# A sandwich of a linear recurrence and a mixture of experts on one core: the softmax's exponentials move from GpSimd to ScalarE, and the first slots are put in another order

## The chip, the cores and the metric

The kernel runs on one core of a Trainium2 chip. The metric is the device time of one execution in microseconds (us); lower is better. The engines are called PE (TensorE, matmuls; PEld is its weight loads), DVE (VectorE), ACT (ScalarE), POOL (GpSimd) and SP (SyncE, which issues most DMAs). Each engine runs its own instructions in the order in which the program has them, and waits for others by semaphores.

## What is computed

The input is 16 blocks of 512 rows and 128 features, all float32. The reference, cut to what matters here:

```python
x = x + layernorm(attn(layernorm(x)))       # per block: Bu = x B^T, a causal convolution along the
                                            # 512 rows with complex eigenvalues, C, and D * x
x = x + layernorm(ffn(layernorm(x)))

# ffn, E = 8 experts, F = 512:
router_probs = softmax(x @ w_router)                 # 8 values for each row
gate_weights = softmax((x @ w_gating) / 0.1)         # 8 values for each row
g = x @ w_gate[e];  u = x @ w_up[e]
out_e = (silu(g) * u) @ w_down[e]
cw = router_probs * gate_weights;  cw = cw / (sum(cw) + 1e-9)
out = sum over e of out_e * cw[e]
```

The softmax of the two routers is what the change touches: for each block of 512 rows it takes 4 x 2 x 8 exponentials in each of 128 partitions.

## The kernel before

**Tiling.** A block is 512 rows, held as 4 chunks of 128. For the experts the features lie on the partitions and the 512 rows along the free dimension. A *slot* is one of the four 128-wide pieces of F of one expert of one block: 4 x 8 = 32 slots a block, 512 slots in all, numbered n. A product of float32 accuracy is made of three matmuls (`mm3`, L337): high part by high part (L338), low part of the weights by high part (L339), and high part by low part (L340). So a slot has nine matmuls of 512 columns: three for g, three for uu (`up`, L554) and, four slots later (LAG), three for d (`down`, L589).

**What the other engines do in a slot.** ACT takes the silu of g from PSUM (`sg`, L564). DVE multiplies it by uu (`gate`, L575); the product stays in uu's PSUM bank, or goes to `hh` in SBUF. ACT rounds the product to its high part (`hi`, L580), and the low part is the difference (`lo`, L586): on DVE, or on POOL where `lo_pool[n]` says so (then the product is in `hh`). Every fourth slot DVE multiplies an expert's d by its combine weights (`ct`, L606) and POOL adds it to the sum (`acc`, L609). PSUM has two banks for g and three for uu, so g(n + 2) can start only after silu(n) has read its bank, and uu(n + 3) only after uu(n) has been read.

**Beside them.** While the slots of one block run, the next block's front part (`front`: two layer norms, the recurrence by a scan on DVE at L381, matmuls bu and yp on PE) and its `route` run as generators, a step at a time, and so does the end of the block before (`back`, with its layer norm and the store). The generator says with each `yield` after how many slots the next step may come and what it costs on DVE, ACT and POOL. In each slot the loop at L807 adds up planned costs in `busy` (an engine gets SLOT = 1.94 us a slot back), and `steps` (L794) lets a step through if `take` (L781) finds room. `lo_pool[n]` (L845) is set where POOL's planned load is below DVE's. So planned costs decide where every step stands, and fewer planned POOL costs put more `lo` on POOL.

**The order of a slot in the program** (L807 to L846) is: hi(n-1) on ACT; g, uu on PE and silu(n) on ACT; d(n-4); ct and acc; the split of the next expert weight (`split_next`, ACT at L110 and POOL at L115) in slots with n % 4 < 3 until all 24 are split; the steps of the generators; lo(n-1); gate(n). Steps on ACT therefore stand between silu(n) and hi(n), and steps on DVE between gate(n-1) and lo(n-1).

**The softmax** (`route`, L408): four small matmuls make the logits `lg` in PSUM, DVE takes the maximum (`mx`, L422) and the difference (`ez`, L424). In block 0 ACT then makes two exponentials (L428, L429). In the other 15 blocks POOL raises the constants e and e^10, held in `bases` (L149 to L151), to the powers `ez`, eight instructions of 128 x 8 for each block (L433), each a step of its own. DVE then sums, divides and multiplies (L436 to L446), and the weights go through DRAM to be spread over the partitions.

**The first slots.** Before the loop, block 0's front part runs by itself with an order written out by hand (L629 to L760). PE makes the low parts of the first three weights (AHEAD = 3; `rest`, L679, whose result ACT copies). Block 0's second layer norm is made in halves: `norm` with `shared` set (L513) puts one chunk on ACT and one on DVE, after DVE has made a small product `nm` (`shift`, L508); PE transposes (L752), ACT makes `xh` and a copy `xT` (L755, L756), DVE makes `xl` (L757). `keep_warm` (L734) puts 9 and 4 matmuls of no use between. The first eight weights (OWN = 8) are loaded into buffers that `hi` and `lo` use later.

Of the kernel before, what the change touches and what calls it, by code (L numbers as in the profile page):

```python
# [2 lines left out]

# [8 lines left out]
F32 = mybir.dt.float32  # L12
F32R = mybir.dt.float32r
# [6 lines left out]
P = 128  # L20
# [4 lines left out]
E = 8  # L25
# [1 line left out]
NF = F // P  # L27
LAG = 4
LEAD = 67
OWN = 8  # L30
WARM = 9, 4, 0
AHEAD = 3
LN_EPS = 1e-5


# [12 lines left out]
def sandwich(ctx, tc, x, a_params, B_w, C_w, Dv, w_router, w_gating, w_gate, w_up, w_down, sines, out):  # L48
# [31 lines left out]
            nc.sync.dma_start(out=xts[b][:, k], in_=x[b].rearrange("(c p) d -> p c d", p=P)[:, k])  # L80


    spare = [hp.tile([P, F], F32R, name=f"spare{i}", tag="lo", bufs=LAG + 1).bitcast(F32) for i in range(2)]

# [51 lines left out]
    dbc = const.tile([P, D], F32, name="dbc")  # L136
    for k in range(AHEAD, OWN):
        load_w(k)
        if k == 4 and NB > 1:
            load_x(1)  # L140
            nc.sync.dma_start(out=dbc, in_=Dv.partition_broadcast(P))

# [3 lines left out]
    gp.memset(neghalf, -0.5)  # L146
    zero = const.tile([P, 1], F32, name="zero")
    gp.memset(zero, 0.0)
    bases = const.tile([P, NT, 2, E], F32, name="bases")  # L149
    gp.memset(bases[:, :, 0], math.e)  # L150
    gp.memset(bases[:, :, 1], math.exp(10.0))  # L151
    cwp = []
    for i in range(2):
        t = const.tile([P, NT, 32], F32, name=f"cwp{i}")
# [13 lines left out]
    def bank(pl, tag, name):  # L168
        return pl.tile([P, T], F32, name=name, tag=tag)
# [176 lines left out]
    def front(b):  # L346
# [58 lines left out]
        vec.tensor_tensor(xl, xT, xh.bitcast(F32), ALU.subtract)  # L405
        blocks[b] = dict(xh=xh, xl=xl, x2=x2, xT=xT)

    def route(b):  # L408

        G2 = NT * 2  # L410
        xT = blocks[b]["xT"]
        yield 1, 0, 0, 0, "f"
        lg = ps_f.tile([P, G2, E], F32, name=f"lg{b}", tag="f")
        for c in range(NT):
            pe.matmul(  # L415
                lg[:, 2 * c : 2 * c + 2], xT[:, P * c : P * c + P], wrg.rearrange("d g e -> d (g e)"),
                start=True, stop=True,
            )
        yield 1, 0.4, 0, 0
        bc = lambda t, n: t.unsqueeze(2).broadcast_to([P, n, E])  # L420
        mx = small.tile([P, G2], F32, name="mx", bufs=2)
        vec.tensor_reduce(mx, lg, AX.X, ALU.max)  # L422
        ez = small.tile([P, G2, E], F32, name="ez", bufs=2)
        vec.tensor_tensor(ez, lg, bc(mx, G2), ALU.subtract)  # L424
        own[0] = False
        if b == 0:
            e4 = ez.rearrange("p (c g) e -> p c g e", g=2)
            act.activation(e4[:, :, 0], e4[:, :, 0], AF.Exp)  # L428
            act.activation(e4[:, :, 1], e4[:, :, 1], AF.Exp, scale=10.0)  # L429
        else:  # L430
            for i in range(G2):
                yield 1, 0, 0, 1.62
                gp.tensor_tensor(ez[:, i], bases.rearrange("p c g e -> p (c g) e")[:, i], ez[:, i], ALU.pow)  # L433
        yield 2, 0.65, 0, 0
        sm = small.tile([P, G2], F32, name="sm", bufs=2)
        vec.tensor_reduce(sm, ez, AX.X, ALU.add)  # L436
        vec.reciprocal(sm, sm)
        vec.tensor_tensor(ez, ez, bc(sm, G2), ALU.mult)
        yield 1, 0.75, 0, 0
        pr = ez.rearrange("p (c g) e -> p c g e", g=2)  # L440
        cw0 = small.tile([P, NT, E], F32, name="cw0", bufs=2)
        vec.tensor_tensor(cw0, pr[:, :, 0], pr[:, :, 1], ALU.mult)
        cs = small.tile([P, NT], F32, name="cs", bufs=2)
        vec.tensor_reduce(cs, cw0, AX.X, ALU.add)
        vec.tensor_scalar(cs, cs, 1e-9, None, ALU.add)
# [186 lines left out]
    def turn(k):  # L632
        for _ in range(k):
            next(rot, None)
# [60 lines left out]
    def state(c):  # L695
        k = quarter[c]
        vec.tensor_tensor(vm[:, k], v[:, k], tre[:, k], ALU.mult)
        pe.matmul(yps[c], vm[:, k], cT, start=False, stop=True)

    vec.tensor_tensor(v[:, left], bus[0], tre[:, left], ALU.mult)  # L700
    turn(2)
    scan(left, 0.0)
    turn(2)
    state(0)
    state(1)
    turn(2)
    vec.tensor_tensor(v[:, right], bus[1], tre[:, right], ALU.mult)
    lo0 = rest(0, ps_u, "u")
    lo0()
    scan(right, v[:, 2 * P - 1 : 2 * P])  # L710
    stat(0, yps[0])
    stat(1, yps[1])
    state(2)
    state(3)
    rest(1, ps_g, "g")()
    r0 = rstd(s6s[0])
    stat(2, yps[2])
    stat(3, yps[3])
    r1 = rstd(s6s[1])
    rest(2, ps_f, "f")()  # L720

# [10 lines left out]
    warm = bank(ps_g, "g", "warm")  # L732

    def keep_warm(k):  # L734
        for _ in range(k):
            pe.matmul(warm, W[0, 0][0][:, :P], W[0, 0][0], start=True, stop=True)

    keep_warm(WARM[0])
    residual(0, r0[1])
    q0 = rstd(s6s[0])  # L740
    residual(1, r1[1])
# [3 lines left out]
    xh = fe.tile([D, T], F32R, name="xh0", tag="xh", bufs=2)  # L745
    xl = fe.tile([D, T], F32R, name="xl0", tag="xl", bufs=2)
    xT = work("ft_x0")
    for h, q in enumerate((q0, q1)):
        norm(halves(xn)[h], halves(x2)[h], q[1], shift(*q), True)
        ps = bank(ps_u, "u", f"xT0{h}")[:, : 2 * P]  # L750
        for i in range(2):
            pe.transpose(ps[:, P * i : P * i + P], xn[:, 2 * h + i], ident)  # L752
        keep_warm(WARM[1 + h])
        k = slice(2 * P * h, 2 * P * h + 2 * P)
        act.copy(xh[:, k], ps)  # L755
        act.copy(xT[:, k], ps)  # L756
        vec.tensor_tensor(xl[:, k], ps, xh[:, k].bitcast(F32), ALU.subtract)  # L757
    for h, r in enumerate((r0, r1)):
        vec.scalar_tensor_tensor(x2m[:, 2 * h : 2 * h + 2], r[0][:, :, 0], -1.0, r[1], ALU.mult, ALU.mult)
    blocks[0] = dict(xh=xh, xl=xl, x2=x2, xT=xT, x2m=x2m)  # L760
    first_route = route(0)

    def first():
# [43 lines left out]
    for n in range(total + LAG):  # L807
        b, s = divmod(n, 32)
        now[0] = n
        busy = [max(0.0, t - SLOT) for t in busy]  # L810
        if n < total:
            take((0.6, 1.0, 0), (9, 9, 9))
        if 0 <= n - 1 < total:
            take((0, 0, 1.23) if lo_pool[n - 1] else (0.6, 0, 0), (9, 9, 9))
            split_hi(n - 1)
        if n < total:
            up(n, *[first] * (n == 0))
        if n == 0:
            begin(n, 0, first_route, 1, routed)
            if NB > 1:  # L820
                begin(n, 1, chain(1), 1)
        if n == 3:
            act.copy(bT[0], bT32)
            gp.tensor_tensor(bT[1], bT32, bT[0].bitcast(F32), ALU.subtract)
        for i in range(NB):
            if i > 1 and n == max(4, 32 * i - LEAD):
                begin(n, i, chain(i))
        m = n - LAG
        if 0 <= m < total:
            down(m)  # L830
        m = n - LAG - (2 if n < total else n == total)
        if m >= 0 and m % 4 == 3:
            take((0.6, 0, 1.23), (9, 9, 9))
            combine(m // 32, m // 4 % 8)
            if m % 32 == 31 and m // 32 in accs:
                begin(n, m // 32 + 0.5, back(m // 32, accs.pop(m // 32)))
        if nsplit < 3 * E and n < total and n % 4 < 3:
            take((0, 0.5, 1.23), (9, 9, 9))
            split_next(1)
        if n < total:  # L840
            steps(n)
        if 0 <= n - 1 < total:
            split_lo(n - 1)
        if n < total:
            lo_pool[n] = busy[2] < busy[0] and n < total - 3  # L845
            gate(n)  # L846


# [25 lines left out]
```

## Time and profile before

| | |
|---|---|
| time, median of 3 runs | 1156.1 us (1156.03 to 1156.17) |
| the profiled execution's own time | 1155.96 us |
| its span, from the first instruction's start to the last one's end | 1154.1 us |
| mean granted TensorE clock | 0.997 |
| start of the first g matmul of slot 0 | 26.4 us |
| start of the first g matmul of slot 32 (block 1) | 106.3 us |
| each of blocks 4 to 12, from first g to the next block's first g | 69.25 us |
| start of the last g (slot 511) | 1141.1 us |
| ACT table loads | 2, of 1.28 us each |

How to read it: the prediction's lines of the page have an engine's busy time, its share of the span and its number of instructions; or a group of instructions by line, engine, operation, output and inputs, shape and count, then busy time and mean nanoseconds of one, then the idle time just before them. A line of a timeline has start and duration in us, engine, line, operation, tiles, shapes and count, and in brackets the idle time before it and who ended it. A line of windows has a stretch, its length, and for each engine busy time and (number of instructions).

### The profile page before, as it was taken

How to read it: one execution, taken by the hardware profiler on the slowest of the kernel's cores; microseconds unless marked ns; L12 is line 12 of the kernel's file. 1: busy time of each engine (PE TensorE's matmuls, PEld its weight loads, DVE VectorE, ACT ScalarE, POOL GpSimd, SP SyncE). 2: the span in 40 equal slices, each digit the busy share in tenths (PEclk: the TensorE clock that was granted, in tenths of full speed). 3: DMA queues.
4: the chain of work that ended last, by engine and by line, in shares of the span. 5: the costliest groups of instructions: out<-in, count | busy, mean ns of one | idle time of the engine just before them, and what ended most of it. 6: DMA issues, size and time to landing. Idle time of an engine off the chain costs nothing.

```text
span 1154.1 us, 16183 instructions
## 1 busy us (share of the span) xinstructions
PE 1131.5 (98%) x4978; PEld 913.3 (79%) x4978; DVE 922.9 (80%) x2101; ACT 698.1 (60%) x1348; POOL 745.6 (65%) x570
## 2 busy tenths in 40 slices
PE   6899999999999999999999999999999999999997
PEld 4678788888888888888888888888888888888885
DVE  6888888887878878787887878888787887868666
ACT  3766656656566655656566565655657566565564
POOL 1679576776757766585866748577585856647442
PEclk9999999999999999999999999999999999999999
DMA  4140312203122131302212130130302202111120
GB/s 152 50 149 4 93 55 56 92 29 92 47 65 64 38 96 43 92 28 74 73 38 83 38 109 29 56 90 30 92 29 81 66 19 74 47 56 28 31 71 10
DMA packets 65894, 71.23 MB, mean 62 GB/s; under 512 B 8624, under 2 KB 50320, under 8 KB 65808
## 3 DMA queue, kind: packets, MB, share of 16 engines
q1 hardware_dynamic: 65392, 70.04, 20.0%
q8 instruction: 39, 0.64, 0.2%
q14 instruction: 47, 0.39, 0.1%
q10 hardware_dynamic: 416, 0.16, 0.1%
HBM read 54.98 MB, written 15.20 MB: 61 GB/s over the span
## 4 chain that ended last, share of the span: by engine, by line
PE 90%; DVE 4%; POOL 3%; issue 2%; ACT 0%; DMA 0%; DVEq 0%; POOLq 0%
PE g L338 10%; PE d L338 10%; PE g L340 10%; PE d L339 10%; PE uu L338 10%; PE d L340 10%; PE uu L340 10%; PE g L339 10%; PE uu L339 9%; PE yp L387 1%; POOL ez L433 1%; PE lg L415 1%; DVE x L302 0%; POOL acc L609 0%; DVE lo L586 0%
## 5 line engine op out<-in xcount | busy, mean ns | idle before, releaser
L586 POOL TENSOR_TENSOR lo<-hh,hi 128x512 fp32r<-128x512 f32 x196 | 261.9, 1336 | 155.1 <-ACT hi L580 155.0
L580 ACT CAST hi<-uu 128x512 fp32r<-128x512 f32 x316 | 185.4, 587 | 244.4 <-DVE uu L575 235.9
L564 ACT ACTIVATE sg<-g 128x512 f32<-128x512 f32 x512 | 306.7, 599 | 17.5 <-PE g L340 11.7
L575 DVE TENSOR_TENSOR uu<-sg,uu 128x512 f32<-128x512 f32 x316 | 218.7, 692 | 93.9 <-ACT sg L564 83.3
L586 DVE TENSOR_TENSOR lo<-uu,hi 128x512 fp32r<-128x512 f32 x316 | 216.9, 687 | 95.9 <-ACT hi L580 93.2
L609 POOL TENSOR_TENSOR acc<-acc,ct 128x512 f32<-128x512 f32 x109 | 142.4, 1306 | 138.9 <-DVE ct L606 89.7
L580 ACT CAST hi<-hh 128x512 fp32r<-128x512 f32 x196 | 121.6, 621 | 162.5 <-DVE hh L575 160.7
L338 PE MATMUL g<-xh,wgh 128*128 128x512 f32 x512 | 206.8, 404 | 2.4 <-ACT sg L564 1.8
L338 PE MATMUL uu<-xh,wuh 128*128 128x512 f32 x512 | 203.9, 398 | 4.3 <-DVE lo L586 4.3
L339 PE MATMUL d<-hi,wdl 128*128 128x512 f32 x512 | 203.3, 397 | 0.0
L340 PE MATMUL g<-xl,wgh 128*128 128x512 f32 x512 | 203.1, 397 | 0.0
L338 PE MATMUL d<-hi,wdh 128*128 128x512 f32 x512 | 203.0, 396 | 0.0
L340 PE MATMUL uu<-xl,wuh 128*128 128x512 f32 x512 | 201.4, 393 | 0.0
L340 PE MATMUL d<-lo,wdh 128*128 128x512 f32 x512 | 201.1, 393 | 0.0
L339 PE MATMUL g<-xh,wgl 128*128 128x512 f32 x512 | 200.8, 392 | 0.0
L339 PE MATMUL uu<-xh,wul 128*128 128x512 f32 x512 | 198.6, 388 | 0.0
L433 POOL TENSOR_TENSOR ez<-bases,ez 128x8 f32<-128x8 f32 x120 | 195.7, 1650 | 0.0
L575 DVE TENSOR_TENSOR hh<-sg,uu 128x512 f32<-128x512 f32 x196 | 133.5, 681 | 12.5 <-ACT sg L564 5.1
L338 PEld LDWEIGHTS g<-xh,wgh 128*128 128x128 f32 x512 | 96.1, 188 | 27.7 <-ACT sg L564 5.2
L338 PEld LDWEIGHTS uu<-xh,wuh 128*128 128x128 f32 x512 | 95.9, 187 | 27.8 <-DVE lo L586 6.0
L339 PEld LDWEIGHTS uu<-xh,wul 128*128 128x128 f32 x512 | 96.4, 188 | 23.8 <-POOL wul L115 0.2
L340 PEld LDWEIGHTS d<-lo,wdh 128*128 128x128 f32 x512 | 96.8, 189 | 22.9
(172 smaller groups left out, 1336.8 us busy)
## 6 DMA issues: line engine op xcount, KB each, us to landing
cwb<-scw SPq DMA_DIRECT2D x64, 512.0 KB
xt<-in_L_attn_u_dram SPq DMA_DIRECT2D x15, 256.0 KB
sco<-ob SPq DMA_DIRECT2D x60, 64.0 KB
ot<-sco SPq DMA_DIRECT2D x15, 256.0 KB
out_dram<-x SPq DMA_DIRECT2D x15, 256.0 KB
scr_u<-blk_u SPq DMA_DIRECT2D x52, 64.0 KB
ft_u<-scr_u SPq DMA_DIRECT2D x13, 256.0 KB
scr_x<-blk_x SPq DMA_DIRECT2D x52, 64.0 KB
```

The source lines that it names most:

```text
L338: pe.matmul(ps, w[0][:, cs], mh, start=first, stop=False)
L339: pe.matmul(ps, w[1][:, cs], mh, start=False, stop=False)
L340: pe.matmul(ps, w[0][:, cs], ml, start=False, stop=last)
L387: pe.matmul(yp[:, c], v[:, P * c : P * c + P], cT, start=True, stop=True)
L415: pe.matmul(lg[:, 2 * c : 2 * c + 2], xT[:, P * c : P * c + P], wrg.rearrange("d g e -> d (g e)"), start=True, stop=True,)
L433: gp.tensor_tensor(ez[:, i], bases.rearrange("p c g e -> p (c g) e")[:, i], ez[:, i], ALU.pow)
L564: act.activation(s, g, AF.Silu)
L575: vec.tensor_tensor(h, s, u, ALU.mult)
L580: act.copy(hi, pend[n])
L586: (gp if lo_pool[n] else vec).tensor_tensor(lo, h, hi.bitcast(F32), ALU.subtract)
L609: add = lambda: eng.tensor_tensor(acc, acc, t, ALU.add)
```

## The change

The exponentials of every block are made by two ACT instructions, as those of block 0 were. The step has a planned ACT cost of 1.6 in place of eight planned POOL costs of 1.62. The constants `bases` go. In the first slots, the order becomes:

- four weights instead of three have their low parts made by PE ahead of the loop (AHEAD = 4), and their four ACT copies come after all four casts; seven weights are loaded ahead (OWN = 7), and block 1's input after them;
- block 0's second norm is all on DVE, chunk by chunk, from mean and inverse deviation, without `nm`; the useless matmuls go; both `xl` follow all four transposes' copies;
- the logits of chunks 0 and 1 are made before g(0), those of 2 and 3 between g(0) and uu(0);
- the first softmax's later steps and the front part of block 1 each start one slot later; the next weight (number 4, expert 1's up) is split in slot 3, then again in slots with n % 4 < 3; no `lo` is put on POOL in slots 0 to 3.

```diff
-OWN = 8
-WARM = 9, 4, 0
-AHEAD = 3
+OWN = 7
+AHEAD = 4
...
-    bases = const.tile([P, NT, 2, E], F32, name="bases")
-    gp.memset(bases[:, :, 0], math.e)
-    gp.memset(bases[:, :, 1], math.exp(10.0))
...
-        if b == 0:
-            e4 = ez.rearrange("p (c g) e -> p c g e", g=2)
-            act.activation(e4[:, :, 0], e4[:, :, 0], AF.Exp)
-            act.activation(e4[:, :, 1], e4[:, :, 1], AF.Exp, scale=10.0)
-        else:
-            for i in range(G2):
-                yield 1, 0, 0, 1.62
-                gp.tensor_tensor(ez[:, i], bases.rearrange("p c g e -> p (c g) e")[:, i], ez[:, i], ALU.pow)
+        if b > 0:
+            yield 1, 0, 1.6, 0
+        e4 = ez.rearrange("p (c g) e -> p c g e", g=2)
+        act.activation(e4[:, :, 0], e4[:, :, 0], AF.Exp)
+        act.activation(e4[:, :, 1], e4[:, :, 1], AF.Exp, scale=10.0)
...
-    keep_warm(WARM[0])
...
-    for h, q in enumerate((q0, q1)):
-        norm(halves(xn)[h], halves(x2)[h], q[1], shift(*q), True)
+    lg = logits(0)
+    for h, (mv, rs) in enumerate((q0, q1)):
         ps = bank(ps_u, "u", f"xT0{h}")[:, : 2 * P]
+        xps.append(ps)
         for i in range(2):
-            pe.transpose(ps[:, P * i : P * i + P], xn[:, 2 * h + i], ident)
-        keep_warm(WARM[1 + h])
-        k = slice(2 * P * h, 2 * P * h + 2 * P)
-        act.copy(xh[:, k], ps)
-        act.copy(xT[:, k], ps)
-        vec.tensor_tensor(xl[:, k], ps, xh[:, k].bitcast(F32), ALU.subtract)
+            c = 2 * h + i
+            vec.tensor_scalar(xn[:, c], x2[:, c], mv[:, i, 0:1], rs[:, i : i + 1], ALU.subtract, ALU.mult)
+            pe.transpose(ps[:, P * i : P * i + P], xn[:, c], ident)
+        act.copy(xh[:, (left, right)[h]], ps)
+        act.copy(xT[:, (left, right)[h]], ps)
+    for h, k in enumerate((left, right)):
+        vec.tensor_tensor(xl[:, k], xps[h], xh[:, k].bitcast(F32), ALU.subtract)
+    score(lg, xT, (0, 1))
...
-            begin(n, 0, first_route, 1, routed)
-            if NB > 1:
-                begin(n, 1, chain(1), 1)
-        if n == 3:
+            begin(n + 1, 0, first_route, 1, routed)
+        if n == 1 and NB > 1:
+            begin(n, 1, chain(1), 1)
+        if n == 4:
...
-        if nsplit < 3 * E and n < total and n % 4 < 3:
+        if nsplit < 3 * E and n < total and (n == 3 or n > 3 and n % 4 < 3):
...
-            lo_pool[n] = busy[2] < busy[0] and n < total - 3
+            lo_pool[n] = busy[2] < busy[0] and 4 <= n < total - 3
```

More of the change, by code (lines that the diff above doesn't have):

```diff
@@ L1 @@
-import math
 from contextlib import ExitStack
@@ L80, in load_x @@
             nc.sync.dma_start(out=xts[b][:, k], in_=x[b].rearrange("(c p) d -> p c d", p=P)[:, k])
-    spare = [hp.tile([P, F], F32R, name=f"spare{i}", tag="lo", bufs=LAG + 1).bitcast(F32) for i in range(2)]
+    spare = [hp.tile([P, F], F32R, name=f"spare{i}", tag="lo", bufs=LAG + 1).bitcast(F32) for i in range(3)]
     raw = {}
@@ L138, in sandwich @@
         load_w(k)
-        if k == 4 and NB > 1:
+        if k == OWN - 1 and NB > 1:
             load_x(1)
@@ L406, in front, with logits, score @@
         blocks[b] = dict(xh=xh, xl=xl, x2=x2, xT=xT)
+    def logits(b):
+        return ps_f.tile([P, NT * 2, E], F32, name=f"lg{b}", tag="f")
+    def score(lg, xT, cs):
+        for c in cs:
+            pe.matmul(
+                lg[:, 2 * c : 2 * c + 2], xT[:, P * c : P * c + P], wrg.rearrange("d g e -> d (g e)"),
+                start=True, stop=True,
+            )
     def route(b):
@@ L412, in route @@
         yield 1, 0, 0, 0, "f"
[L413 to L418, printed above, removed]
+        if b > 0:
+            lg = logits(b)
+            score(lg, xT, range(NT))
+        else:
+            lg = blocks[0]["lg"]
+            score(lg, xT, (2, 3))
         yield 1, 0.4, 0, 0
@@ L425, in route @@
         own[0] = False
-        if b == 0:
-            e4 = ez.rearrange("p (c g) e -> p c g e", g=2)
-            act.activation(e4[:, :, 0], e4[:, :, 0], AF.Exp)
-            act.activation(e4[:, :, 1], e4[:, :, 1], AF.Exp, scale=10.0)
-        else:
-            for i in range(G2):
-                yield 1, 0, 0, 1.62
-                gp.tensor_tensor(ez[:, i], bases.rearrange("p c g e -> p (c g) e")[:, i], ez[:, i], ALU.pow)
+        if b > 0:
+            yield 1, 0, 1.6, 0
+        e4 = ez.rearrange("p (c g) e -> p c g e", g=2)
+        act.activation(e4[:, :, 0], e4[:, :, 0], AF.Exp)
+        act.activation(e4[:, :, 1], e4[:, :, 1], AF.Exp, scale=10.0)
         yield 2, 0.65, 0, 0
@@ L700, in sandwich @@
     vec.tensor_tensor(v[:, left], bus[0], tre[:, left], ALU.mult)
+    lo = [rest(0, ps_u, "u")]
     turn(2)
@@ L705, in sandwich @@
     state(1)
+    lo.append(rest(1, ps_f, "f"))
     turn(2)
     vec.tensor_tensor(v[:, right], bus[1], tre[:, right], ALU.mult)
-    lo0 = rest(0, ps_u, "u")
-    lo0()
     scan(right, v[:, 2 * P - 1 : 2 * P])
@@ L714, in sandwich @@
     state(3)
-    rest(1, ps_g, "g")()
+    lo.append(rest(2, ps_g, "g"))
     r0 = rstd(s6s[0])
@@ L719, in sandwich @@
     r1 = rstd(s6s[1])
-    rest(2, ps_f, "f")()
+    lo.append(rest(3, ps_g, "g"))
+    for f in lo:
+        f()
     x2 = fe.tile([P, NT, D], F32, name="x20", tag="x2", bufs=3)
@@ L730, in residual @@
             stat(c, x2[:, c])
[L732 to L736, printed above, removed]
-    keep_warm(WARM[0])
     residual(0, r0[1])
@@ L747, in sandwich @@
     xT = work("ft_x0")
-    for h, q in enumerate((q0, q1)):
-        norm(halves(xn)[h], halves(x2)[h], q[1], shift(*q), True)
+    xps = []
+    lg = logits(0)
+    for h, (mv, rs) in enumerate((q0, q1)):
         ps = bank(ps_u, "u", f"xT0{h}")[:, : 2 * P]
+        xps.append(ps)
         for i in range(2):
-            pe.transpose(ps[:, P * i : P * i + P], xn[:, 2 * h + i], ident)
-        keep_warm(WARM[1 + h])
-        k = slice(2 * P * h, 2 * P * h + 2 * P)
-        act.copy(xh[:, k], ps)
-        act.copy(xT[:, k], ps)
-        vec.tensor_tensor(xl[:, k], ps, xh[:, k].bitcast(F32), ALU.subtract)
-    for h, r in enumerate((r0, r1)):
-        vec.scalar_tensor_tensor(x2m[:, 2 * h : 2 * h + 2], r[0][:, :, 0], -1.0, r[1], ALU.mult, ALU.mult)
-    blocks[0] = dict(xh=xh, xl=xl, x2=x2, xT=xT, x2m=x2m)
+            c = 2 * h + i
[6 more added lines that the diff above has]
+    score(lg, xT, (0, 1))
+    for h, (mv, rs) in enumerate((r0, r1)):
+        vec.scalar_tensor_tensor(x2m[:, 2 * h : 2 * h + 2], mv[:, :, 0], -1.0, rs, ALU.mult, ALU.mult)
+    blocks[0] = dict(xh=xh, xl=xl, x2=x2, xT=xT, x2m=x2m, lg=lg)
     first_route = route(0)
@@ L825, in sandwich @@
         for i in range(NB):
-            if i > 1 and n == max(4, 32 * i - LEAD):
+            if i > 1 and n == max(10, 32 * i - LEAD):
                 begin(n, i, chain(i))
```

## The prediction

> **What bounds the kernel now.** I read the page's table of engines first, then TensorE (PE) by stages, then the timelines of ScalarE (ACT), VectorE (DVE) and GpSimd (POOL) around the two places that the change touches.
>
> ```profile
> PE 1131.5 (98%) x4978; PEld 913.3 (79%) x4978; DVE 922.9 (80%) x2101; ACT 698.1 (60%) x1348; POOL 745.6 (65%) x570
> L433 POOL TENSOR_TENSOR ez<-bases,ez 128x8 f32<-128x8 f32 x120 | 195.7, 1650 | 0.0
> ```
> ```profile
> core 0: us, PE busy (x) PEld busy (x) DVE busy (x) ACT busy (x) POOL busy (x), PEclk, DMA share, GB/s
> 26.40:106.30 79.90, 74.17 (x323) 57.55 (x324) 65.93 (x138) 55.40 (x110) 59.06 (x46) 0.98 0.24 73
> 592.40:661.60 69.20, 69.20 (x308) 56.39 (x307) 57.76 (x122) 41.81 (x80) 46.70 (x35) 1.00 0.22 65
> ```
> The second fence holds two stages, block 0 and block 8. In block 8 PE is busy for the whole 69.2 us: its matmuls start 0.232 us apart, nine to a slot of 2.087 us, and blocks 4 to 12 each take 69.25 us from first g to first g. There nothing can be won by unloading another engine: the 195.7 us of powers that leave POOL are worth **nothing by themselves**. Block 0 takes 79.9 us, and 26.4 us pass before it. So a gain can come only from the first 106 us, and the steady blocks can only lose, where ACT's new work makes PE wait.
>
> **How near a wait the steady blocks are.** A slot is a loop: silu (ACT), product (DVE), hi (ACT), the next silu. Slots 306 to 309 show what happens when it is disturbed; first ACT, then DVE, then POOL:
>
> ```profile
> 701.73 0.60 ACT L564 ACTIVATE sg<-g 128x512 f32<-128x512 f32 x1
> 702.23 1.27 ACT L298 ACTIVATE x<-x,nm 128x128 f32<-128x128 f32 x4
> 703.40 0.57 ACT L580 CAST hi<-uu 128x512 fp32r<-128x512 f32 x1
> 703.86 0.61 ACT L564 ACTIVATE sg<-g 128x512 f32<-128x512 f32 x1
> 707.09 0.59 ACT L580 CAST hi<-uu 128x512 fp32r<-128x512 f32 x1 [2.62 <-DVE uu L575]
> 707.58 0.60 ACT L564 ACTIVATE sg<-g 128x512 f32<-128x512 f32 x1
> 709.04 0.59 ACT L580 CAST hi<-uu 128x512 fp32r<-128x512 f32 x1 [0.86 <-DVE uu L575]
> 709.52 0.61 ACT L564 ACTIVATE sg<-g 128x512 f32<-128x512 f32 x1
> ```
> ```profile
> 703.02 1.65 DVE L302 SCALAR_TENSOR_TENSOR x<-ot,rs,x 128x128 f32<-128x128 f32 x2
> 704.60 1.22 DVE L381 TENSOR_TENSOR_SCAN v<-v,zero 128x512 f32<-128x512 f32 x1
> 705.74 0.66 DVE L586 TENSOR_TENSOR lo<-uu,hi 128x512 fp32r<-128x512 f32 x1
> 706.32 0.68 DVE L575 TENSOR_TENSOR uu<-sg,uu 128x512 f32<-128x512 f32 x1
> ```
> ```profile
> 703.11 1.42 POOL L379 TENSOR_TENSOR du<-u,dbc 128x512 f32<-128x512 f32 x1
> ```
> The silu at 707.58 starts 1.77 us after its g is finished; I call that its lateness. The next ones are 1.94 us apart, so lateness falls by 2.087 - 1.942 = 0.145 us a slot, and by 0.7 to 0.8 us more where bu, lg or yp makes a PE slot longer (2.78, 2.89 and 2.90 us). PE does not feel it until lateness reaches about 2.65: slot 356 had 2.54, and its silu still ended 0.18 us before g(358) overwrote the buffer. The highest lateness of blocks 4 to 12 is 1.8 to 2.5. The slack is nearly used already, but no wait results.
>
> **The exponentials: +20 us.** In each of blocks 1 to 15 the changed program's order has on ACT: silu(n), table load, exp, exp, hi(n), table load, silu(n+1). The trace has one such switch, in block 0:
>
> ```profile
> 29.00 0.23 ACT L428 ACTIVATE ez<-ez 128x32 f32<-128x32 f32 x1 [2.36 <-DVE ez L424]
> 29.14 0.21 ACT L429 ACTIVATE ez<-ez 128x32 f32<-128x32 f32 x1
> 29.36 1.28 ACT L564 ACT_TABLE_LOAD   x1
> 30.66 0.60 ACT L564 ACTIVATE sg<-g 128x512 f32<-128x512 f32 x1
> ```
> A load takes 1.28 + 0.02 us, the two exps 0.36. Ahead of hi that is 1.66, of which 0.85 lies in ACT's idle time there (the 0.86 above). The second load stands between hi and silu, where nothing is idle, and costs 1.30 plus the 0.1 by which silu now starts before hi ends. So each block's silus are made 0.81 + 1.40 = 2.21 us later, against a slack of 2.65 that other bursts use too. Queued behind: hi (so lo, and d four slots on) and the silu that frees g's buffer, for which PE waits.
>
> Whether PE waits depends on what stands near. I keep a ledger by slot: lateness rises by the larger of (ACT's extra work - 0.85) and (DVE's extra work - 0.74, or - 1.34 where lo is on POOL), and falls as above; what passes 2.65 is a PE wait. DVE's extras go by the rows' spacing (a 512-wide product 0.60, scan 1.20, residual 0.27, statistics 0.21, small ones 0.13 to 0.20). Beside a 512-wide POOL instruction DVE's SBUF-only rows are longer: L302 0.34 to 1.40 us, the nm of L286 0.15 to 1.14, the scan 1.22 to 2.35; beside the powers L302 stays at 0.34. I price that at up to 0.45 for a residual, 0.9 for a scan, 0.8 for xl and 0.25 for a small one, times a share c. On the kernel as it is, c = 0.5 gives a mean lateness of 0.82 over slots 64 to 469 (measured 0.80) and no wait in blocks 4 to 12 (measured none); c = 0 gives 0.28, and c = 0.8 gives waits that aren't there.
>
> Block 10 of the changed order with c = 0.5: lateness is 0.42 at slot 14. The exps: +2.21 - 0.145 = 2.49. Slot 15 gives 2.34. In slot 16 DVE has ct, nm, the four cw/cs rows and the scan: 2.66 + 1.07 of lengthening - 1.34 = +2.39, less 0.145: 4.59, of which 1.94 is a wait. Slot 18 (four residual biases on ACT, +0.43) adds 0.14; yp takes 0.81 off in slot 19. Wait: **2.1 us**, with c = 0 0.7. The order repeats every three blocks: exps in slot 14, 15 or 17, residual burst in 18 or 19; waits 2.13, 1.89, 1.54 with c = 0.5 and 0.68, 0.71, 0.10 with c = 0. Blocks 2 to 15 sum to 20.6 and 5.2 (0.4 and 0.2 on the old order), so +20.2 or +5.0; c = 0.8 gives +29. I take **+20**, as c = 0.5 is the share that the trace bears out. Against it: POOL's 512-wide lo rise from 196 to 254 by the order, which lengthens more DVE rows; for it: DVE has 58 lo fewer, which the ledger holds already.
>
> The Trainium skill ("ScalarE: Activation LUTs", What ACT_TABLE_LOAD costs) has 2.66 us for a switch, 1.38 of it a drain. In this trace the load starts 0.01 us after the exp ends, and no drain shows. By the page a block would lose 2.8 us more, an estimate of some 36 us over the kernel; by the row, nothing more.
>
> **The first slots: -1.9 us.** Now DVE's last statistics end at 21.32 and POOL's power at 22.10, but the second half's normalisation starts at 24.97, behind 13 warming matmuls on PE, and xl and nm on DVE; then transposes 25.52, g 26.41, its third matmul 27.15, lg to 28.44, exp 29.00, silu(0) 30.66. Changed: DVE makes the four normalisations without nm, the third at 22.16; transposes end near 23.3, xh 23.7, copy 24.0, xl 24.45, third matmul 24.5, half of lg 0.5, maximum and difference 0.7, exps 0.36, load 1.30: silu(0) at 27.7. PE idles from about 18.7 to 21.7 and isn't kept warm; matmuls at half pace (below) add 0.5: 28.2, 2.5 earlier. Then the loop sets the pace, 1.97 a slot: silu(3) at 34.1. Only then does ACT cast weight 4 (0.62; expert 1's up), and POOL makes its low part (1.30): 36.6. The second matmul of uu(4) waits for that; g(5) follows five matmuls later, at 37.75, now 39.60: **-1.85**. From there PE is full. Bounds: cold PE again and a late cast, -0.4; none of it, -2.8. The first cost nothing before, as three casts in slots 0 to 2 did it: that is the wait that replaces them. What a cold PE costs shows after a 2.57 us wait: matmuls start 0.43 apart, not 0.23, seven times, 1.4 us:
>
> ```profile
> 75.05 0.79 PE L338 MATMUL uu<-xh,wuh 128*128 128x512 f32 x1 [2.17 <-DVE lo L586]
> 75.64 0.63 PE L339 MATMUL uu<-xh,wul 128*128 128x512 f32 x1
> ```
> The SP queue moves weight 3 ahead of the router's two loads and block 1's x behind weights 4 to 6, half a microsecond an issue; x is first read at about 28, so this is covered.
>
> **Rest of blocks 0 and 1: -2 us.** From g(7) at 44.30 to g(32) at 106.28 are 62.0 us; 25 x 2.087 and 4.3 of other matmuls make 56.5, so 5.5 are lost, most where four L302 beside weight splits took 3.2 us, and 0.9 in block 1. The new order halves that burst but has the exps in slot 29: by the ledger (c = 0.5) 4.2 in both. From -5 to +3.
>
> **Sum.** 1155.96 of the profiled execution (span 1154.1, median of three 1156.1) + 20.2 - 1.85 - 2.2 = 1172.1: **1172 us**.
>
> **The rivals.**
> 1. *The slack takes it; the first slots decide (faster).* DVE gives up 58 lo, blocks' peaks stay under 2.65, and PE keeps its 0.232 us. Then only the front speaks: 1156 - 1.9 - 2.2 = 1152. It decides if the lengthening of DVE rows is no larger than at c = 0 and bursts miss each other; for it, today's peaks never cost anything; against it, three of three slot patterns pass 2.65 even at c = 0.
> 2. *They cancel:* c near 0, 5 us of waits against 4 won: 1157.
> 3. *The reorder does not do what it says:* uu(4) waits for the late weight and a cold PE, block 0 wins nothing; with the exps 1176, inside the forecast's own range.
> 4. *More contention:* POOL's extra lo take c to 0.8 or over: 1156 + 37 - 3 = 1190.
>
> **How the numbers follow.** Forecast with rival 3: 0.65, own range 1161 to 1185. Rival 1: 0.17. Rival 2: 0.10, most of it within 0.2% (2.3 us, about what a measurement here can tell from no change). Rival 4: 0.08. Low end 1153, inside rival 1, high end 1188. Faster by over 0.2% 0.16, within 0.08, slower 0.76.
>
> **What would show it.** Blocks 4 to 12 at 70 to 71.5 us, not 69.25, with PE waits of 0.1 to 2 us before g (released by sg) or uu, one to six slots after each table load: right. Blocks at 69.25: the ledger is wrong, rival 1. Table rows longer than 1.28, or idle time behind them: the page was right. g(5) at 37 to 38.5 and matmuls 0.43 apart near 24 to 28: the front is right. Every loss at the residual bursts, none at the loads: DVE's lengthening, not ACT, is the cause.

## The result, and the profile after

The changed kernel takes **1175.9 us** (median; 1175.5 to 1177.5) against 1156.1 beside it: a ratio of 1.017, 95% interval 1.0153 to 1.0188. It is slower, by more than the 0.2% that can be told from no change; 1172 was predicted. The profiled execution took 1177.46 us (span 1175.7), 21.5 more than that of before; it was the slowest of the four, so the sums by stages below come out 1.6 us above the median.

The first fence has two lines of the page after, the second the stages of blocks 0 and 8, from first g to first g:

```profile
PE 1143.2 (97%) x4969; PEld 913.0 (78%) x4969; DVE 878.0 (75%) x2043; ACT 731.2 (62%) x1407; POOL 625.5 (53%) x505
L588 POOL TENSOR_TENSOR lo<-hh,hi 128x512 fp32r<-128x512 f32 x254 | 339.5, 1337 | 264.1 <-ACT hi L582 264.1
```
```profile
core 0: us, PE busy (x) PEld busy (x) DVE busy (x) ACT busy (x) POOL busy (x), PEclk, DMA share, GB/s
24.28:110.48 86.20, 77.88 (x311) 59.72 (x311) 59.34 (x135) 57.00 (x111) 50.15 (x40) 0.92 0.23 71
606.27:677.25 70.98, 70.41 (x308) 55.90 (x307) 55.05 (x120) 44.47 (x86) 37.45 (x30) 1.00 0.19 55
```
DVE is 45 us less busy and POOL 120, and the kernel is slower: neither was the bound. Block 8 now has 0.57 us in which PE does nothing; the rest of its 1.7 us more is in matmuls that start late but overlap the last one's modelled end. Block 0 is 6.3 us longer, at a granted clock of 0.92.

By stages, in us, from the starts of the g matmuls (L333; L338 before). A block's length runs to the next block's first g:

| kernel (profiled) | first g | block 0 | block 1 | blocks 2-13 | blocks 4-12, each | span |
|---|---|---|---|---|---|---|
| before | 26.42 | 79.87 | 70.23 | 831.8 | 69.25 | 1154.1 |
| after | 24.28 | 86.20 | 71.72 | 847.7 | 70.5 to 71.0 | 1175.7 |
| e1 exponentials only | 26.42 | 79.24 | 70.18 | 848.7 | 70.5 to 71.2 | 1171.6 |
| e2 front only | 24.38 | 86.18 | 70.74 | 839.6 | 69.2 to 69.5 | 1166.7 |
| e3 no loads | 24.87 | 83.05 | 70.90 | 834.2 | 69.2 to 70.1 | 1159.1 |
| e4 POOL plan | 24.15 | 86.16 | 70.22 | 839.5 | 69.25 (6 to 12) | 1166.0 |
| e5 weights early | 23.83 | 81.31 | 70.51 | 846.2 | 70.2 to 71.0 | 1167.9 |
| e6 lo on DVE | 23.92 | 85.42 | 71.68 | 857.3 | 70.6 to 72.4 | 1184.1 |
| e7 map (old kernel) | 26.43 | 79.59 | 70.24 | 840.8 | 69.25 to 71.8 | 1162.9 |
| e8 exponentials late | 24.93 | 84.49 | 71.71 | 853.1 | 70.9 to 71.2 | 1180.2 |
| e9 both | 24.38 | 82.03 | 70.25 | 840.6 | 69.25 | 1163.4 |
| e10 front, powers | 24.87 | 82.27 | 69.35 | 843.1 | 69.2 to 69.3 | 1165.4 |
| e11 priced | 23.79 | 81.32 | 70.55 | 843.6 | 69.4 to 70.5 | 1165.7 |
| e12 priced, old front | 26.55 | 79.39 | 70.14 | 846.3 | 70.5 to 70.8 | 1168.5 |

The change, summed: -2.1 to the first g, +6.3 in block 0, +1.5 in block 1, +15.9 in blocks 2 to 13, nothing behind them: +21.5. Block 0 isn't the same in every execution: in the four other kernels with these first slots, these late weights and these loads (e2, e4, e6, e8) it took 84.49 to 86.18 us. (The 17.6 in the first expectation below is a slip of addition; 15.9 is right.)

**Where a steady block loses.** ACT, then DVE, POOL and PE of the changed kernel, slots 305 to 312 (the residual's rows, L302 in the kernel before, are L297 here):

```profile
717.46 1.28 ACT L434 ACT_TABLE_LOAD   x1
718.75 0.23 ACT L434 ACTIVATE ez<-ez 128x32 f32<-128x32 f32 x1
718.89 0.21 ACT L435 ACTIVATE ez<-ez 128x32 f32<-128x32 f32 x1
719.01 0.57 ACT L582 CAST hi<-uu 128x512 fp32r<-128x512 f32 x1
719.60 1.28 ACT L566 ACT_TABLE_LOAD   x1
720.89 0.60 ACT L566 ACTIVATE sg<-g 128x512 f32<-128x512 f32 x1
```
```profile
726.51 0.68 DVE L608 TENSOR_TENSOR ct<-d,cwb 128x512 f32<-128x512 f32 x1
727.11 1.67 DVE L297 SCALAR_TENSOR_TENSOR x<-ot,rs,x 128x128 f32<-128x128 f32 x2
```
```profile
727.34 1.29 POOL L611 TENSOR_TENSOR acc<-acc,ct 128x512 f32<-128x512 f32 x1 [0.96 <-DVE ct L608]
```
```profile
729.79 0.39 PE L335 MATMUL d<-lo,wdh 128*128 128x512 f32 x1
730.97 0.50 PE L333 MATMUL g<-xh,wgh 128*128 128x512 f32 x1 [0.78 <-ACT sg L566]
```
The silu before the load was 1.47 us late, the one at 720.89 is 3.42 (its g ended at 717.47). PE does not wait yet, as yp's longer slot comes next, and lateness falls to 2.53. Then two rows of L297 take 1.67 us, where 0.60 is usual: POOL's sum began at 727.34, 0.03 us ahead of the second of them. Lateness is 3.61, and g(312) waits: its matmul starts 1.18 us behind the one before it, not 0.23. In the pattern of block 10 the lengthened row behind the loads is the scan, with 2.17 us where 1.20 is usual, and PE waits 1.3 us at g of slot 20.

**Where block 0 loses.** PE at uu(4):

```profile
35.72 0.49 PE L333 MATMUL uu<-xh,wuh 128*128 128x512 f32 x1 [1.41 <-ACT wuh L108]
37.09 0.50 PE L334 MATMUL uu<-xh,wul 128*128 128x512 f32 x1 [0.87 <-POOL wul L113]
37.91 0.63 PE L334 MATMUL d<-hi,wdl 128*128 128x512 f32 x1
38.76 0.63 PE L333 MATMUL g<-xh,wgh 128*128 128x512 f32 x1
```
Both waits are for weight 4, and seven matmuls after them start 0.43 us apart, at a granted clock of 0.50: g(5) starts at 38.76, 0.84 earlier than before, and g(7) at 44.46, 0.16 later. Further on, the second matmuls of g(16), uu(16) and uu(24) start 1.42, 0.69 and 1.05 us behind the one before them, each because of a weight's late low part. The largest wait at the end of block 0 is of another kind: g(32) starts 1.86 us behind the matmul before it, because the silu that frees its bank, that of slot 30, stands behind the second table load of block 1's exponentials.

```profile
66.54 0.50 PE L334 MATMUL g<-xh,wgl 128*128 128x512 f32 x1 [1.02 <-POOL wgl L113]
...
110.47 0.50 PE L333 MATMUL g<-xh,wgh 128*128 128x512 f32 x1 [1.47 <-ACT sg L566]
```
In e3, without these loads, g(32) starts 0.46 us behind the matmul before it.

### The profile page after: what moved, and what is told of

Its sections match the earlier page's. It is cut to its first block, busy times and chain, and to the rows that moved or that the text cites. A ratio compares the mean times of both kernels' runs of the same rounds, so it can differ in the third digit from the quotient of the medians.

```text
span 1175.7 us, 16106 instructions
## 1 busy us (share of the span) xinstructions
PE 1143.2 (97%) x4969; PEld 913.0 (78%) x4969; DVE 878.0 (75%) x2043; ACT 731.2 (62%) x1407; POOL 625.5 (53%) x505
## 5 line engine op out<-in xcount | busy, mean ns | idle before, releaser
L588 POOL TENSOR_TENSOR lo<-hh,hi 128x512 fp32r<-128x512 f32 x254 | 339.5, 1337 | 264.1 <-ACT hi L582 264.1
L577 DVE TENSOR_TENSOR uu<-sg,uu 128x512 f32<-128x512 f32 x258 | 178.8, 693 | 161.1 <-ACT sg L566 155.3
L582 ACT CAST hi<-hh 128x512 fp32r<-128x512 f32 x254 | 157.5, 620 | 220.1 <-DVE hh L577 213.9
L582 ACT CAST hi<-uu 128x512 fp32r<-128x512 f32 x258 | 151.1, 585 | 187.8 <-DVE uu L577 182.2
L588 DVE TENSOR_TENSOR lo<-uu,hi 128x512 fp32r<-128x512 f32 x258 | 177.1, 687 | 88.1 <-ACT hi L582 83.2
L611 POOL TENSOR_TENSOR acc<-acc,ct 128x512 f32<-128x512 f32 x109 | 143.0, 1312 | 165.7 <-DVE ct L608 127.3
L333 PE MATMUL g<-xh,wgh 128*128 128x512 f32 x512 | 210.4, 411 | 9.8 <-ACT sg L566 8.8
L333 PE MATMUL uu<-xh,wuh 128*128 128x512 f32 x512 | 205.1, 401 | 4.9 <-DVE lo L588 3.4
L333 PE MATMUL d<-hi,wdh 128*128 128x512 f32 x512 | 203.1, 397 | 0.0
L577 DVE TENSOR_TENSOR hh<-sg,uu 128x512 f32<-128x512 f32 x254 | 172.2, 678 | 16.9 <-issue 7.3
L333 PEld LDWEIGHTS g<-xh,wgh 128*128 128x128 f32 x512 | 96.6, 189 | 44.3 <-ACT sg L566 22.9
L333 PEld LDWEIGHTS uu<-xh,wuh 128*128 128x128 f32 x512 | 96.4, 188 | 31.6 <-DVE lo L588 5.6
L335 PEld LDWEIGHTS g<-xl,wgh 128*128 128x128 f32 x512 | 96.9, 189 | 23.5 <-DVE xl L757 0.2
```

Of the source, the lines that this page charges most:

```text
L333: pe.matmul(ps, w[0][:, cs], mh, start=first, stop=False)
L335: pe.matmul(ps, w[0][:, cs], ml, start=False, stop=last)
L577: vec.tensor_tensor(h, s, u, ALU.mult)
L582: act.copy(hi, pend[n])
L588: (gp if lo_pool[n] else vec).tensor_tensor(lo, h, hi.bitcast(F32), ALU.subtract)
L611: add = lambda: eng.tensor_tensor(acc, acc, t, ALU.add)
```

## The experiments

**e1: the exponentials alone**, in the kernel before (its first slots kept):
```diff
-        if b == 0:
...
-            for i in range(G2):
-                yield 1, 0, 0, 1.62
-                gp.tensor_tensor(ez[:, i], bases.rearrange("p c g e -> p (c g) e")[:, i], ez[:, i], ALU.pow)
+        if b > 0:
+            yield 1, 0, 1.6, 0
+        e4 = ez.rearrange("p (c g) e -> p c g e", g=2)
+        act.activation(e4[:, :, 0], e4[:, :, 0], AF.Exp)
+        act.activation(e4[:, :, 1], e4[:, :, 1], AF.Exp, scale=10.0)
```


> The exponentials alone: ScalarE computes them for every block, with the table loads around them; the first slots stay as in the kernel before. If the exponentials cause the loss of the steady blocks (my theory), blocks 4 to 12 are 70.5 to 71 us as in the changed kernel, blocks 2 to 13 lose some 17.6 us, and the time is 1174 (1171 to 1177). If the loss comes from the reordered first slots (rival: they shift everything behind them), blocks 4 to 12 are back at 69.25 and the time is within 1155 to 1160.

Measured: 1173.5 us, ratio 1.014 (1.0123 to 1.0157). Blocks 2 to 13 lose 16.9 us, 14 another 1.2; blocks 0 and 1 gain 0.7. The exponentials make the steady loss, whatever the first slots are.

**e2: the front alone**, ScalarE's exponentials in blocks 0 and 1, powers from block 2 on:
```diff
+        if b < 2:
             if b > 0:
                 yield 1, 0, 1.6, 0
...
+        else:
+            for i in range(G2):
+                yield 1, 0, 0, 1.62
+                gp.tensor_tensor(ez[:, i], bases.rearrange("p c g e -> p (c g) e")[:, i], ez[:, i], ALU.pow)
```


> The first slots as in the changed kernel, with ScalarE's exponentials in blocks 0 and 1 only; GpSimd's powers come back for blocks 2 to 15. If front and exponentials add up, blocks 2 to 13 are back to 69.25 to 69.7 us and what is left is the front (first g 2.1 earlier), block 0 (+6.3) and block 1 (+1.5): 1161.5 (1160 to 1163). By the prediction's terms (front and rest of blocks 0 and 1 together -4.1) it would be 1152. If block 0's loss is a consequence of what follows in blocks 2 and on, it would be under 1157.

Measured: 1167.2, ratio 1.0083 (1.0067 to 1.0098). Up to block 1's first g 4.3 us are lost, as in the changed kernel (4.2), block 1 loses 0.5, and blocks 3 to 15 are back but for 0.3. The other 7.6 us stand in block 2, and were not foreseen: with the chain of eight powers the combine weights are transposed for their way through DRAM at 197.6, in the changed kernel at 183.7, and come late. DVE of this kernel, slot 75:

```profile
208.64 0.69 DVE L612 TENSOR_TENSOR acc<-d,cwb 128x512 f32<-128x512 f32 x1 [4.83 <-DMA cwb<-scw]
```
So the two halves of the change are not independent: with the new first slots the powers' chain ends too late for block 2.

**e3: no table loads**:
```diff
+        f = AF.Identity if b > 0 else AF.Exp
-        act.activation(e4[:, :, 0], e4[:, :, 0], AF.Exp)
-        act.activation(e4[:, :, 1], e4[:, :, 1], AF.Exp, scale=10.0)
+        act.activation(e4[:, :, 0], e4[:, :, 0], f)
+        act.activation(e4[:, :, 1], e4[:, :, 1], f, scale=10.0)
```


> The changed kernel with the exponentials of blocks 1 to 15 replaced by ScalarE's identity (times 1 and times 10) at the same places, so that no table has to be loaded; this leaves the exponentials of those blocks out, the planner's order is unchanged, and the two short ACT rows and GpSimd's 254 low parts stay. If the two loads of 1.28 us cause the waits (my theory), only 0.36 us a block is left of ACT's extra work, blocks 4 to 12 are 69.25 to 69.5 us, and the time is 1158 (1156 to 1162). If VectorE's lengthening beside GpSimd's additional low parts causes them (rival), blocks 4 to 12 stay at 70.5 to 71 and the time is 1174 or more.

Measured, with the exponentials of blocks 1 to 15 left out: 1160.9, ratio 1.0031 (1.0021 to 1.0041). Blocks 2 to 13 lose 2.4 us instead of 15.9, with the same order and 254 low parts on POOL. The loads are needed for the loss; POOL's additional low parts alone do not make it.

**e4: POOL planned as if it still had the powers**:
```diff
+    def ghost():
+        for _ in range(2 * NT):
+            yield 1, 0, 0, 1.62
...
             yield 1, 0, 1.6, 0
+            begin(now[0], b + 0.25, ghost())
```


> The changed kernel, but GpSimd's share of the low parts is planned as if the powers were still on it: 190 low parts there rather than 254 (196 in the kernel before), the rest on VectorE. Table loads as in the changed kernel. If the loads cause the loss, it stays: 1176 (1172 to 1181), since VectorE has some 64 low parts more again, 0.6 us each where VectorE is late. If VectorE's lengthening beside GpSimd's additional 512-wide rows is the cause, blocks 4 to 12 fall to 69.25 to 69.7 and the time to 1162 or less.

Measured: 1167.4, ratio 1.0082 (1.0067 to 1.0097), between the two expectations. Blocks 6 to 12 are 69.25 us *with* all loads. So the loads alone do not make it either. Blocks 2 to 5 and 13, in other slot patterns, lose 7.7. From block 2 on, rows of L297 longer than 0.4 us (up to 1.42) stand in blocks 2, 4, 5 and 13 alone; blocks 6 to 12 have none.

**e5: weights split in the slots of the kernel before**:
```diff
-        if nsplit < 3 * E and n < total and (n == 3 or n > 3 and n % 4 < 3):
+        if nsplit < 3 * E and n < total and (n in (1, 2) or n > 3 and n % 4 < 3):
```


> The changed kernel, but ScalarE and GpSimd split the weights from number 4 on in the same slots as in the kernel before (4 in slot 1, 5 in slot 2, 6 in slot 4, then three slots of four), not one to two slots later. If block 0's loss comes from weights that are a slot late (uu(4) 3.2 us and a cold PE 1.4, g(16) and its uu 1.9, slots 23 and 24 1.9), block 0 falls from 86.2 us to 79 to 81 and the time from 1176 to 1170 (1168 to 1172). If another step of block 0 is as late by itself (the norms and splits on ACT and DVE between slots 1 and 30), the waits only move and the time stays at 1174 to 1177.

Measured: 1169.6, ratio 1.0114 (1.0099 to 1.013): 6.3 less than the changed kernel. g(5) starts at 34.35 instead of 38.76, block 0 is 81.31, and block 2's first g at 175.65, 0.9 earlier than before. PE at the same place:

```profile
33.13 0.40 PE L334 MATMUL uu<-xh,wul 128*128 128x512 f32 x1
...
34.35 0.50 PE L333 MATMUL g<-xh,wgh 128*128 128x512 f32 x1
```

**e6: the low parts of slots 18 to 25 on DVE**:
```diff
+    def on_gp(n):
+        return lo_pool[n] and not (n >= 64 and 18 <= n % 32 <= 25)
...
-        if lo_pool[n]:
+        if on_gp(n):
...
-        (gp if lo_pool[n] else vec).tensor_tensor(lo, h, hi.bitcast(F32), ALU.subtract)
+        (gp if on_gp(n) else vec).tensor_tensor(lo, h, hi.bitcast(F32), ALU.subtract)
```


> The changed kernel with its planner's order, but from block 2 on the low parts of slots 18 to 25 of each block, some 4 of them on GpSimd, are made on VectorE (193 left on GpSimd instead of 254). Table loads unchanged. If VectorE's lengthening beside GpSimd's 512-wide rows right after the loads takes the rest of the slack, blocks 4 to 12 fall by 0.5 to 1.3 us each and the time to 1165 (1162 to 1170). If the loads alone cause the waits, moving work of 0.6 us a piece onto VectorE makes blocks 4 to 12 equal or longer (70.6 to 71.5), time 1176 to 1184.

Measured: 1186.1, ratio 1.0254 (1.0239 to 1.0269). Worse by 10: blocks of two patterns rise to 71.8 and 72.1 to 72.4, the third stays at 70.65. Taking those low parts off POOL doesn't help, and the 61 rows that DVE gets instead cost time, so this run doesn't tell what the lengthening beside them is worth by itself. The longest L297 rows stay at 1.4 us: in blocks 4 to 12 the POOL row beside most of them is the sum L611.

**e7: one more pair of exponentials, in the kernel before, at different slots**:
```diff
+    def probe(n):
+        at = {3: 27, 4: 8, 5: 8, 6: 14, 7: 14, 8: 17, 9: 17, 10: 21, 11: 21, 12: 27}
+        if at.get(n // 32) == n % 32:
+            for i in range(2):
+                act.activation(dummy[:, 2 + i], dummy[:, i], AF.Exp)
...
+            probe(n)
```


> The kernel before, with its powers on GpSimd, and one extra pair of exponentials of a scratch tile on ScalarE, so two table loads, in each of ten blocks, at different slots: slot 27 in blocks 3 and 12, 8 in blocks 4 and 5, 14 in 6 and 7, 17 in 8 and 9, 21 in 10 and 11. The scan lies in slot 15 of the even and 18 of the odd blocks, the residual burst in 18 and 19. If the waits come from loads that meet the bursts, blocks with 14 and 17 lose 0.5 to 2 us and those with 8, 21 and 27 under 0.3: 1160 (1157 to 1163). If a pair of loads costs a wait wherever it stands, each of the ten loses 1 to 1.5 us: 1168 or more. If only GpSimd's additional low parts make the loads felt, none loses anything: 1156 to 1157.

Measured: 1165.1, ratio 1.0071 (1.0056 to 1.0086). The map is not the one expected: slots 14 and 17 cost 0.0 to 0.5 us, slot 21 0.7 and 0.5, slot 8 2.6 and 0.3, slot 27 0.7 and 2.6. What counts is the lateness that stands there: in slot 130 it was 2.63 instead of 1.19, left from the pair of slot 123; at the pair of slot 136 it was 2.25, and the next silu was 4.21 late.

**e8: the exponentials behind the residual burst**:
```diff
-            yield 1, 0, 1.6, 0
+            yield (1 if b < 3 else max(1, 32 * b - 10 - now[0])), 0, 1.6, 0
```


> The changed kernel, but from block 2 on the exponentials wait until slot 22, behind the residual burst of slots 18 to 20, instead of standing in slots 14 to 17 ahead of it. As many table loads, and 260 low parts on GpSimd. If the loads cost only where they meet the scan and the residual burst within some four slots, blocks 4 to 12 fall to 69.3 to 70 us and the time to 1166 (1162 to 1170). If the loads cost wherever they are, or GpSimd's low parts are the cause, blocks stay at 70.5 to 71: 1175 to 1178.

Measured: 1181.9, ratio 1.0217 (1.02 to 1.0234): worse. The waits now come at g of slot 28 and uu of slot 31, at the next burst. Moving the loads away from one burst moves them onto another.

**e9: e4 and e5 together.**

> The changed kernel with both corrections: weights split in the slots of the kernel before, and GpSimd's share of the low parts planned as if the powers were still there (VectorE's rows around the exponentials less dense). All table loads stay. If the two losses are separate, block 0 is 81.3 us, block 1 70.2, blocks 5 to 12 69.25 (a load that meets a lateness under 0.75 us costs nothing), and the time 1159 (1157 to 1162). If the loads still cost where the pattern of slots is another, blocks 4 to 12 are 70 or more and the time is 1166 or more.

Measured: 1165.2, ratio 1.0067 (1.0054 to 1.0079). Blocks 4 to 12 are 69.25 us, all nine; block 1 is 70.25, block 0 82.0. The total was missed, because blocks 2, 3 and 13 lose 4.7, 2.2 and 1.9 us in patterns that don't repeat. Block 8's stage, its loads (ACT) and its residual rows (DVE):

```profile
599.45:668.70 69.25, 69.25 (x309) 56.41 (x307) 54.76 (x126) 44.89 (x87) 33.18 (x26) 1.00 0.20 62
```
```profile
638.72 1.28 ACT L439 ACT_TABLE_LOAD   x1
640.85 1.28 ACT L571 ACT_TABLE_LOAD   x1
642.15 0.60 ACT L571 ACTIVATE sg<-g 128x512 f32<-128x512 f32 x1
```
```profile
649.71 0.61 DVE L297 SCALAR_TENSOR_TENSOR x<-ot,rs,x 128x128 f32<-128x128 f32 x2
```
The loads raise lateness from 0.74 to 2.69, by 1.95 us; in the changed kernel's slot 305 it was 1.95 too. The price is the same; here it meets a lower lateness, and L297 then takes 0.61, not 1.67. In blocks 4 to 12 no row of L297 is longer than 0.4 us; blocks 2, 3 and 13, which lose, have rows of up to 1.41.

**e10: e2 with early weights**, and the later chains from slot 4:
```diff
-            if i > 1 and n == max(10, 32 * i - LEAD):
+            if i > 1 and n == max(4, 32 * i - LEAD):
```


> The changed kernel's first slots, with weights split in the slots of the kernel before, ScalarE's exponentials in blocks 0 and 1 only, GpSimd's powers from block 2 on, and the chains of the later blocks begun from slot 4 on as in the kernel before, not from slot 10. If the front's gain is what is left of it at g(32) when the weights are early (1.1 us) and nothing else changes, blocks 2 to 15 are as before and the time is 1155 (1153.5 to 1156.5): at most 0.2 per cent under the kernel before. If the later chains still come too late for block 2, there is a wait of 1 to 8 us near slot 75, and the time is 1157 to 1163.

Measured: 1167.1, ratio 1.0082 (1.0068 to 1.0096), above both expectations. The wait at slot 75 is there still: DVE stands idle for 8.89 us there, and block 2 takes 80.35. The powers start in slot 58, as in the kernel before, and yet the combine weights are transposed in slot 71 rather than 69. So the chain's start is not the cause; what delays its later steps stays open.

**e11: the exponentials priced on every engine**, with early weights:
```diff
-            yield 1, 0, 1.6, 0
+            yield ((1, 1.6, 1.6, 1.2) if b > 1 else (1, 0, 1.6, 0))
```


> The changed kernel with weights split in the slots of the kernel before, and the planner told that the exponentials of blocks 2 to 15 also take 1.6 us of VectorE and 1.2 us of GpSimd (before: 1.6 us of ScalarE alone). They move behind the scan and the first half of the residual burst, to slot 20, with less put behind them; 250 low parts stay on GpSimd, and all table loads stay. If the wait comes from what the planner packs around the loads, blocks 4 to 12 are 69.25 to 69.5 us and the time is 1155 (1153 to 1158). If GpSimd's additional low parts, or the loads by themselves, cost the time, blocks 4 to 12 stay above 70.3 and the time is 1167 or more.

Measured: 1168.2, ratio 1.01 (1.0081 to 1.0118). A miss: blocks 4 to 12 are 70.5 us, each waiting at slot 31, except block 8 with 69.44. All nine have the same order of instructions. DVE and then POOL, in blocks 8 and 9:

```profile
663.97 0.60 DVE L297 SCALAR_TENSOR_TENSOR x<-du,rs,xt 128x128 f32<-128x128 f32 x2
...
733.40 1.67 DVE L297 SCALAR_TENSOR_TENSOR x<-du,rs,xt 128x128 f32<-128x128 f32 x2
```
```profile
664.49 1.29 POOL L611 TENSOR_TENSOR acc<-acc,ct 128x512 f32<-128x512 f32 x1 [0.88 <-DVE x L297]
...
733.63 1.29 POOL L611 TENSOR_TENSOR acc<-acc,ct 128x512 f32<-128x512 f32 x1 [0.58 <-DVE ct L608]
```
In block 8 DVE's rows came first, POOL started behind them, and lateness ended at 2.66: no wait. In block 9 POOL started between the two rows: 1.07 us more, lateness 3.73, and PE waits 1.05. This is the clearest reading of the study: same order, same loads, and one lengthened row decides.

**e12: the same price, old first slots.**

> The kernel before with ScalarE's exponentials for every block, priced for the planner as in the run beside it (1.6 us of ScalarE and VectorE, 1.2 us of GpSimd from block 2 on), and the old first slots. Against the run beside it this tells what the new first slots with early weights are worth: first g is 2.0 to 2.6 us later here, block 0 some 2 us shorter, so I expect 1156 (1154 to 1159), 0 to 1.5 us more than beside it. If the new first slots bring nothing, both are equal or this one is faster.

Measured: 1170.7, ratio 1.0122 (1.0104 to 1.014), 2.5 above e11, where 0 to 1.5 was expected. Only 0.4 of that stands at block 2's first g (176.07 against 175.66). With early weights that g starts 0.9 us before the unchanged kernel's 176.52 in e5 and e11, but at 176.49 in e10 and 176.66 in e9, where the granted clock between g(0) and g(2) was 0.54 and 0.50 instead of 1.00. So the new first slots are worth from nothing to 0.9 us. No kernel of the study is faster than the one before.

## Why the prediction was nearly right

**What bounds the kernel: right.** With 120 us off POOL, blocks 14 and 15 are unchanged and no steady block is under 69.2 us.

**The exponentials, +20.2: the mechanism right, the size 4 too large.** The rows are as priced (31 loads of 1.28, started 0.02 us behind the row before; no drain). A switch was to add 2.21 less 0.145; measured 1.95. The blocks were to take 70 to 71.5 us and take 70.5 to 71.0; by pattern the waits were to be 2.13, 1.89 and 1.54 and are 1.4, 1.7 and 1.3. PE waits one to six slots behind the loads, as predicted, and in one of the three patterns once more at slot 31. The sign set for another cause, every loss at residual bursts and none at the loads, did not show as such: the loss needs both. Without loads 2.4 us of 15.9 remain (e3); without a lengthened row behind them the loads cost 0 to 0.2 us a block (e9, e11's block 8).

What failed in the ledger is the share c. Worked out again for the later orders (estimates, made after the runs), it gives 27, 11 and 24 us for blocks 2 to 13 of e6, e7 and e8, where 25.5, 9.0 and 21.3 were measured; but on e4 25.7 against 7.7, and on e11 2.1 against 11.9. A row is not lengthened by a share: a residual row takes 0.34 us, or, if a POOL row of 512 columns has started, it ends 0.15 us behind that row, so in up to 1.4. An average over bursts serves an average over patterns, and tells little of a single pattern.

**The first slots, -1.85: not kept.** First g came 2.1 earlier and silu(0) at 28.8, not 28.2: the cold PE cost more than the 0.5 put in for it (in e5, e6 and e11, where the clock stayed at 1.00, silu(0) is at 27.6 to 27.7, as the prediction had it without that 0.5). The late weight was seen (36.6 predicted, 37.1 measured), but not that the two waits for it would leave PE at half pace for seven matmuls, 1.4 us. So -0.84 at g(5) and nothing at g(7).

**Rest of blocks 0 and 1, -2.2: this step failed.** Measured from g(5) to block 2's first g: +6.5. The working priced one late weight, number 4, and let the ledger do the rest, where weights count as work and not as due times. In the new order every weight from 4 to 23 is split a slot or two later; so uu(4), g(16), uu(16) and uu(24) wait. (The waits before the uu of slots 20 and 23 are for DVE's low parts, and are there in e5 too.) The other term that was too small is block 1's exponentials in slot 29, with 1.6 us at g(32). With the old slots one weight is still waited for, at uu(16), 0.76 us behind the matmul before it, and blocks 0 and 1 with the front come to -0.9 (e5), against -4.05 predicted. Rival 3 named the late weight, but only the first; that its 1176 is the measured time is luck, as it had the exponentials 4 too dear and these blocks 5.7 too cheap.

**The sum.** The exponentials were overpriced by 4, front and first blocks underpriced by 10 (+5.7 against -4.05). The two errors partly cancel; that the time came out nearer than its terms is luck.

**What stays open.** Which property of e9's order frees its blocks, the lateness of 0.74 rather than 1.47 that the loads meet, or the L297 rows that miss POOL's sum. e11's pair shows that the second alone can decide; e9 has both. Whether an order without the losses of e9's blocks 2, 3 and 13 would pass below 1156 was not tried.

## What to carry to other kernels

- Where the bound engine has slack of a fixed size, add up what spends it: a cost that fits alone (two table loads, 2.0 us) and another that fits alone (a lengthened row, 1.07 us) make a wait together. Look at the lateness that stands where the new work lands, not at the engine's mean load.
- When a reordering moves one step, write down the due time of every later item in the same queue. Here the first late weight was found and the nineteen behind it were not; two slots among theirs, 16 and 24, made PE wait.
- A planner's price steers more than the work it stands for: the same exponentials cost 0 to 1.9 us a block (e9, e8) by what it put around them, and moving or repricing them by reasoning (e8, e11) did not find the free place; pretending that POOL was still busy (e4) did, for blocks 6 to 12.

## What the runs showed of the hardware

- Whether DVE and POOL meet is a race, not a rate. A residual row takes 0.34 us alone. When it starts while a 512-wide row of POOL (1.29) runs, it ends some 0.15 us behind that row: in the changed kernel it takes 1.41 us when POOL started 0.03 us ahead, 0.78 at 0.71 ahead, 0.38 at 1.06 ahead. Of 468 such rows in the fourteen traces 458 end 0.14 to 0.17 us behind POOL's. In e11's block 8 POOL's row came second and stood idle for 0.88 us, until L297. The Trainium skill (SBUF — State Buffer, section "SBUF: two separate sides") says that VectorE and GpSimd share ports that one instruction locks for its whole length, whichever starts first; among the VectorE instructions that need them it names those with two SBUF inputs, as L297 has, where GpSimd's instruction reads SBUF. These rows agree.
- PE's clock at the start varies between executions. With the new first slots first g came at 23.8 to 24.9 us, and g(2) 4.45 us behind it in three profiled executions (e5, e6, e11), with a granted clock of 1.00 between them, and 6.0 to 6.1 behind it in the seven others, at 0.50 to 0.55. With the warming matmuls of the kernel before, first g came within 26.4 to 26.6 in four kernels, and g(2) 4.9 behind it in three of them, at 1.00, and 6.6 in the fourth (e7), at 0.58.
- Two matmuls that started 1.80 and 1.37 us behind the one before them were followed by 3.4 us at a granted clock of 0.50, seven matmuls at half pace, and so they were in e2, e4 and e6 (1.78 to 1.88 and 1.36 to 1.38); in e3 and e8, with 1.46 to 1.50 and 1.37, the clock stayed at 1.00.
